# Two-group ending of each GraphSAGE layer's last half, with sums in four PSUM banks, early aggregation of the other batch-norm statistics, and some maskings moved behind the batch norm

## Chip, cores and metric

One Trainium2 chip, one core. The metric is device time in microseconds (us) of one execution; the time before is the median of 3 runs.

## What is computed

The input is x (16 graphs, 1024 nodes, 128 features), an adjacency matrix of 1024 x 1024 per graph and a node mask. Two layers, each with a residual: x = x + layer(relu(layernorm(x))). The first is masked multi-head attention. The second is a GraphSAGE stack of three layers over a thinned ("dilated") adjacency; its core in the reference is

```python
def _sage(x, adj, Wr, Wx, b, mf):
    deg = jnp.clip(jnp.sum(adj, axis=-1, keepdims=True), 1.0, None)
    agg = jnp.einsum('bij,bjd->bid', adj, x) / deg
    out = agg @ Wr + x @ Wx + b
    nrm = jnp.maximum(jnp.linalg.norm(out, axis=-1, keepdims=True), NORM_EPS)
    return out / nrm * mf[..., None]

def _bn(x, g, b):
    m = jnp.mean(x, axis=(0, 1))
    v = jnp.var(x, axis=(0, 1))
    return (x - m) * jax.lax.rsqrt(v + BN_EPS) * g + b
...
h1 = _bn(jax.nn.relu(_sage(x, adj_d, Wr1, Wx1, b1, mf)), g1, be1)
h2 = _bn(jax.nn.relu(_sage(h1, adj_d, Wr2, Wx2, b2, mf)), g2, be2)
h3 = _bn(jax.nn.relu(_sage(h2, adj_d, Wr3, Wx3, b3, mf)), g3, be3)
xc = jnp.concatenate([h1, h2, h3], axis=-1) * mf[..., None]
return (xc @ Wl + bl) * mf[..., None]
```

The batch norm takes mean and variance over all 16 graphs and 1024 nodes, so no row of a layer can enter the next one before the last row's statistics are known. That is the point in the program that the change rewrites, three times, once per layer.

## The kernel before, in words

The function `swept` does all the work here (a second function, `walked`, runs only when a flag says that the first one's way of thinning has not settled; the profile shows none of it). Up to about 2340 us it computes the attention and the thinning of the adjacency, and leaves the transposed adjacency (`aT_d`, f32) and the marks of removed edges (`mr_d`, bf16) in HBM. Then come the three GraphSAGE layers (L = 0, 1, 2, called first, second and third layer in the text), and behind them a tail that adds the third layer's part of the output.

A layer is a loop over 16 graphs (b) with two halves (c = 0, 1) of 512 nodes each; one half is a turn. In a turn i the generator `nodes` (L1107) makes, in this order:

- the half's own product h @ Wx with the bias in PSUM (`own`, L1118), copied to SBUF by ScalarE (`mine`, L1123);
- the sums over neighbours, aT.T @ y with y = h @ Wr (y is written by `given`, L1098, product `pn`, L1103): four tiles of 128 nodes, eight products each, in the PSUM tile `pg` of two banks, two tiles to a bank (L1132). In the first layer a column of ones in y gives the degree too;
- the ending: 1/degree (L1143 and L1146, first layer only), `o = pg / degree + mine` (L1150, one instruction per tile), the squares of all four tiles on ScalarE (L1155), their sums (L1158), maximum (L1160), root on ScalarE (L1161), reciprocal and node mask (L1163, L1164), relu times factor (L1165), four transposes by TensorE into the bank `pt` (L1169), statistics for the batch norm (`bn_stats`, L1176, or L1172 for the last half) and a copy to SBUF (`hT`, L1173).

The ending of one half is spread over the turn of the next one. The order on TensorE, VectorE and ScalarE is written out by hand in the loop from L1230 on (`tc.manual_schedule`): generators stop at named points, and `go(before, "norm")` runs the ending of the half before up to such a point between two blocks of sums (`go(this, "sums")`). Among them stand the four maskings of the next turn's adjacency (`pieces`, L146, VectorE: aT is set to zero where an edge was removed; each takes two of the eight blocks of rows), the next graph's batch norm (`incoming`, L1096, ScalarE) and products. In the second and third layer, turns with c = 1 also add the finished layer's part of the output (`output_part`, products L1059, additions L1064); for the last two graphs these four parts are kept back until the layer's end (`held`, `last_parts`), where TensorE has nothing else to do.

SP's queue loads each turn's adjacency (`edges`, L133, 2 MB into one of four buffers) and marks (L137, two of 512 KB into one of four buffers each) up to three turns ahead; a load waits until its buffer's last reader is done, and those behind it in the queue wait too. Its order, and that of GpSimd's queue (`sums_so_far`, the stores of partial outputs), is the scheduler's.

At a layer's end (L1318 to L1336) the last half's ending runs with nothing beside it but the held products. Then `bn_aggr` takes all 32 groups of statistics (L1325), ScalarE the root (L1328), and VectorE makes scale and shift (`affine`, L1329 to L1332). The next layer begins with the batch norm of graph 0 (`incoming`, both halves on ScalarE), `given` for both halves, and its first turn. After the third layer the tail (from L1338) loads the partial outputs, and per graph takes the batch norm (`come`), eight products (L1364), eight additions (six on VectorE, L1372, two by way of ScalarE, L1401, and VectorE, L1385) and two stores by SP (L1378).

PSUM tags in the text: `sc` is the tile of two banks (two buffers: `pg` lives there), `o`, `t`, `n` and `y` are single banks for `own`, `pt`, `pn` and the output parts.

## Time and profile before

| | |
|---|---|
| median of 3 runs | 3398.16 us (3393.99, 3398.16, 3398.21) |
| the profiled execution's own time | 3396.91 us |
| its span, first to last instruction | 3395.1 us |
| mean granted clock of TensorE | 0.995 |
| TensorE, VectorE, ScalarE busy | 98%, 89%, 68% |
| DMA, mean over the span | 227 GB/s |
| last sums to next layer's first sums, first to second layer | 2649.4 to 2665.0 us |
| the same, second to third layer | 2994.9 to 3007.8 us |
| last sums of the third layer to the tail's first addition | 3336.3 to 3349.9 us |

How to read it: a line of the timeline gives start, duration, engine, line of the kernel, operation, what is written from what, shape and count, and in brackets how long the engine had been idle before and what released it. PE is TensorE, DVE is VectorE, ACT is ScalarE, SP the queue that issues most DMAs. A line of windows gives a stretch, its length, and the busy time of each engine with the number of instructions, then the clock that TensorE was granted (1.00 is full), the share of the DMA engines that was busy, and GB/s. Matmuls in f32 count two records per product, transposes one. Shares of busy time are means over stages with different limits; what a change at a layer's end is worth is read there.

### The profile page before, as it was taken

How to read it: one execution, taken by the hardware profiler on the slowest of the kernel's cores; microseconds unless marked ns; L12 is line 12 of the kernel's file. 1: busy time of each engine (PE TensorE's matmuls, PEld its weight loads, DVE VectorE, ACT ScalarE, POOL GpSimd, SP SyncE). 2: the span in 40 equal slices, each digit the busy share in tenths (PEclk: the TensorE clock that was granted, in tenths of full speed). 3: DMA queues.
4: the chain of work that ended last, by engine and by line, in shares of the span. 5: the costliest groups of instructions: out<-in, count | busy, mean ns of one | idle time of the engine just before them, and what ended most of it. 6: DMA issues, size and time to landing. Idle time of an engine off the chain costs nothing. (4 is left out here: it accounts for less than half of the span.)

```text
span 3395.1 us, 86338 instructions
## 1 busy us (share of the span) xinstructions
PE 3310.6 (98%) x34855; PEld 1872.4 (55%) x34855; DVE 3025.5 (89%) x5399; ACT 2305.4 (68%) x3909; POOL 164.2 (5%) x253
## 2 busy tenths in 40 slices
PE   8999999999999999999999999999999899999997
PEld 3333333333333333333334334336999899999997
DVE  7898989989989998998998999897888899988887
ACT  7699689779879969968976986884232344423334
POOL 2000000000000000000000000000000000000000
PEclk9999999999999999999999999999999999999999
DMA  7357456547637736845863773677999799989996
GB/s 242 108 168 206 137 149 199 161 129 221 188 122 213 221 122 183 238 144 158 236 190 122 237 240 119 189 228 261 346 341 343 284 353 350 353 323 350 352 351 222
DMA packets 650123, 772.28 MB, mean 227 GB/s; under 512 B 173264, under 2 KB 569168, under 8 KB 637424
## 3 DMA queue, kind: packets, MB, share of 16 engines
q1 hardware_dynamic: 632672, 708.58, 64.4%
q0 software_dynamic: 15456, 57.30, 5.0%
q8 instruction: 275, 4.51, 0.6%
q14 instruction: 136, 1.11, 0.1%
q10 hardware_dynamic: 1584, 0.79, 0.1%
HBM read 508.50 MB, written 157.29 MB: 196 GB/s over the span
## 5 line engine op out<-in xcount | busy, mean ns | idle before, releaser
L603 DVE TENSOR_TENSOR w<-e,aT 128x1024 f32<-128x1024 f32 x1024 | 1205.5, 1219 | 138.4 <-ACT e L598 136.8
L598 ACT ACTIVATE e<-sc 128x1024 f32<-128x1024 f32 x1024 | 991.9, 1022 | 333.6 <-PE sc L560 332.6
L1132 PE MATMUL pg<-y,aT 128*128 128x128 f32 (+1 forms) x6144 | 729.8, 275 | 0.0
L1132 PEld LDWEIGHTS pg<-y,aT 128*128 128x128 f32 x6144 | 707.9, 192 | 0.0
L487 PE MATMUL acc<-w,both 128*32 128x512 f32 x4096 | 586.7, 605 | 3.1 <-DVE w L603 2.6
L560 PE MATMUL sc<-qT,kT 32*128 32x512 f32 x4096 | 584.4, 640 | 0.3 <-ACT qT L315 0.3
L492 PE MATMUL acc<-e,eps 128*32 128x512 f32 x4096 | 573.1, 592 | 0.0
L146 DVE SCALAR_TENSOR_TENSOR aT<-mr,aT 128x1024 f32<-128x1024 bf16 x384 | 458.8, 1217 | 0.0
L492 PEld LDWEIGHTS acc<-e,eps 128*32 128x32 f32 x4096 | 150.6, 110 | 294.6 <-issue 289.6
L1155 ACT ACTIVATE sq<-o 128x512 f32<-128x512 f32 x96 | 60.6, 631 | 328.5 <-DVE o L1150 328.5
L554 PEld LDWEIGHTS <-never 32*32 32x32 bf16 x8192 | 80.9, 88 | 347.9 <-issue 325.6
L554 PE MATMUL sc<-nomask,never 32*32 32x512 bf16 x8192 | 252.3, 385 | 16.8 <-ACT e L598 12.3
L1173 ACT COPY hT<-pt 128x512 f32<-128x512 f32 x96 | 56.3, 586 | 289.3 <-PE pt L1169 280.0
L560 PEld LDWEIGHTS sc<-qT,kT 32*128 32x128 f32 x4096 | 160.1, 183 | 116.9 <-issue 116.1
L505 PEld LDWEIGHTS pa<-ident,a 128*128 128x128 f32 x1024 | 107.7, 141 | 181.4 <-issue 129.7
L487 PEld LDWEIGHTS acc<-w,both 128*32 128x32 f32 x4096 | 92.8, 108 | 156.2 <-issue 65.4
L915 ACT ACTIVATE wr<-both,th 128x512 f16<-128x512 f16 x256 | 172.1, 730 | 7.1 <-DVE both L900 6.9
L505 PE MATMUL pa<-ident,a 128*128 128x128 f32 x1024 | 168.3, 287 | 6.4 <-DMA a<-in_adj 5.7
L512 ACT ACTIVATE nomask<-aT 128x512 bf16<-128x512 f32 x256 | 161.4, 630 | 8.1
L1150 DVE SCALAR_TENSOR_TENSOR o<-pg,rdeg,mine 128x128 f32<-128x128 f32 x384 | 108.1, 344 | 55.9 <-PE pg L1132 52.6
L508 ACT COPY aT<-pa 128x512 f32<-128x512 f32 x256 | 152.7, 597 | 5.3 <-PE pa L505 4.3
L900 DVE TENSOR_TENSOR_SCAN both<-rk 128x513 f16<-128x513 bf16 x128 | 155.9, 1218 | 0.0
(228 smaller groups left out, 3894.9 us busy)
## 6 DMA issues: line engine op xcount, KB each, us to landing
aT<-aT_d SPq DMA_DIRECT2D x94, 2048.0 KB, 9.9
mr<-mr_d SPq DMA_DIRECT2D x188, 512.0 KB, 6.0
aT_d<-aT SPq DMA_DIRECT2D x256, 256.0 KB, 4.0
a<-in_adj SPq DMA_DIRECT2D x253, 256.0 KB, 3.7
ad<-in_adj SPq DMA_DIRECT2D x112, 512.0 KB, 4.2
nomask<-nomask SPq DMA_DIRECT2D x512, 96.0 KB, 2.7
nomask<-nomask SPq DMA_DIRECT2D x512, 64.0 KB, 2.7
nomask<-nomask SPq DMA_DIRECT2D x512, 32.0 KB, 2.7
```

The costliest lines, as they stand in the source:

```text
L146: nc.vector.scalar_tensor_tensor(part, mrs[h][:, j : j + 2, :].rearrange("p j n -> p (j n)"), 0.0, part, ALU.is_equal, ALU.mult)
L487: nc.tensor.matmul(acc[g][32 * j : 32 * j + 32, :], v1[:, m, (2 * j + g) * HW : (2 * j + g) * HW + 32], ws[j // 2][:, j % 2, :], start=(m ...
L492: nc.tensor.matmul(acc[g][32 * j : 32 * j + 32, :], eps8, es[j // 2][:, j % 2, :], start=False, stop=(m == NB - 1),)
L505: nc.tensor.transpose(pa[:, k * P : (k + 1) * P], a[:, k, :], ident)
L512: nc.scalar.activation(nomask[:, 0, :], aT[:, 0, :], AF.Relu, bias=1.0, scale=-1e38, accum_out=zeros[:, i : i + 1])
L554: nc.tensor.matmul(scs[j // 2][to : to + 32, j % 2, :], never[rows, rows], nomask[rows, j, :], start=True, stop=False, tile_position=(32 * ...
L560: nc.tensor.matmul(scs[j // 2][:, j % 2, :], kT[rows, mm], qTs[c][rows, g, :], start=False, stop=True, tile_position=(32 * j, 0),)
L598: nc.scalar.activation(e, scs[q], AF.Exp, scale=1.0 / math.sqrt(HD))
L603: nc.vector.tensor_tensor(w, es[q], aT.to_broadcast([P, 2, HN]), ALU.mult)
L900: nc.vector.tensor_tensor_scan(pair_sums[b % 2], row[:, 0::2], row[:, 1::2], 0.0, ALU.add, ALU.add)
L915: nc.scalar.activation(wrs[b][:, t * HN : (t + 1) * HN], pair_sums[b % 2][:, t : t + HN], AF.Abs, bias=at[:, b : b + 1], scale=2.0,)
L1132: nc.tensor.matmul(pg[:, i // 2, at : at + width], aT[:, j, i * P : (i + 1) * P], y[:, j, :width], start=(j == 0), stop=(j == NB - 1),)
```

## The change

- The last turn of a layer (graph 15, c = 1) has its four tiles' sums in four different banks instead of two: the two of `pg`, one of the other `sc` buffer, and `y`.
- Its ending is a new generator, `ending`, in two groups of two tiles. Tiles 0 and 1 are scaled after the second block of sums, tile 2 after the third, and the first group is normed while TensorE works on the last block; tile 3 follows. Squares and their sums come from one instruction per tile with an accumulator (ScalarE for tiles 0 to 2, VectorE for tile 3). Each group has its own two transposes and its own statistics.
- The half before it (c = 0 of graph 15) is normed, transposed and counted earlier in that turn; then its and all other halves' statistics, 31 groups, are aggregated (`most`) and multiplied with their share of the rows. After the last two groups' statistics, the two results are combined by formula (share 1 - 0.5/16).
- Of the four maskings of the next layer's first turn, three (end of the first layer) or two (end of the second) are moved from the last turn behind the affine (`owed`). The third layer's end has none.
- The batch norm of the next layer's graph 0 (`arrive`) is made right there, the first half in two quarters on ScalarE, the second half on VectorE. One of the four held output parts is added before the owed maskings, three after.
- The held parts 2 and 3 of the products share one `sc` tile (`late["pair"]`) instead of taking two.
- At the end of the first layer, where there are no held parts, TensorE makes 14 and then 18 transposes of the identity into an unused bank (`running`).
- The constant `bn_eps` and its memset go: epsilon is in `most`.

On SP's queue two loads change places: at the end of the first layer the adjacency of turn 35 now stands ahead of the marks of turn 34, and at the end of the second one load of marks stands one place later. Away from the layer ends every engine has the same order as before.

The core of the diff (left out: the removal of `bn_eps`, the tile sizes of `stats` and `two`, and `come(0)`, which `arrive` replaces):

```diff
     banks = {"n": (ps_d, "d"), "o": (ps_o, "acc0"), "t": (ps_o, "acc1"), "y": (ps_m, "m")}
 
     def bank(name, tag):
+        if tag in (0, 1):
+            if tag == 0:
+                late["pair"] = ps_s.tile([P, 2, 512], F32, name=name, tag="sc")
+            return late["pair"][:, tag, :]
         if tag == "g":
             return ps_s.tile([P, 2, 512], F32, name=name, tag="sc")[:, 0, :]
         where, tag = banks[tag]
...
             cc = slice(c * HN, (c + 1) * HN)
             nc.scalar.activation(hT[:, cc], hTs[b][:, cc], AF.Identity, bias=affine[:, 1:2], scale=affine[:, 0:1])
 
+    def arrive(hT, b, affine):
+        for cc in (slice(0, HN // 2), slice(HN // 2, HN)):
+            nc.scalar.activation(hT[:, cc], hTs[b][:, cc], AF.Identity, bias=affine[:, 1:2], scale=affine[:, 0:1])
+        nc.vector.tensor_scalar(hT[:, HN:], hTs[b][:, HN:], affine[:, 0:1], affine[:, 1:2], ALU.mult, ALU.add)
+
     def given(L, b, c, hT, tag="n"):
 
         pn = bank(f"pn_{L}_{b}_{c}", tag).rearrange("p (k d) -> p k d", d=D)
...
 
         mine = evict() if late else None
         pg = ps_s.tile([P, 2, 512], F32, name=f"pg_{L}_{b}_{c}", tag="sc")
+        if last_half:
+            pgs = [pg[:, 0, :], pg[:, 1, :], bank(f"pg_{L}_2", "g"), bank(f"pg_{L}_3", "y")]
+        else:
+            pgs = [pg[:, i // 2, (i % 2) * (D + 1) :] for i in range(HB)]
         for i in range(HB):
             for j in range(NB):
-                at = (i % 2) * (D + 1)
                 nc.tensor.matmul(
-                    pg[:, i // 2, at : at + width], aT[:, j, i * P : (i + 1) * P], y[:, j, :width],
+                    pgs[i][:, :width], aT[:, j, i * P : (i + 1) * P], y[:, j, :width],
                     start=(j == 0), stop=(j == NB - 1),
                 )
             yield "sums"
+            if last_half and i == 1:
+                end = ending(L, k0, pgs, mine)
+                go(end, "first group")
+            if last_half and i == 2:
+                go(end, "third block")
+        if last_half:
+            yield from end
+            return
         if not mine:
             mine = evict()
             yield "mine"
...
         pt = bank(f"pt_{L}_{b}_{c}", "t")
         for i in range(HB):
             nc.tensor.transpose(pt[:, i * P : (i + 1) * P], o[:, i, :], ident)
-        last_half = b == B - 1 and c == 1
-        if last_half:
+        if b == B - 1:
             nc.vector.bn_stats(late["stats"][:, 2 * b + c, :], pt)
         nc.scalar.copy(hTs[b][:, c * HN : (c + 1) * HN], pt)
         yield "transposed"
-        if not last_half:
+        if b < B - 1:
             nc.vector.bn_stats(late["stats"][:, 2 * b + c, :], pt)
         yield "end"
+
+    def ending(L, k0, pgs, mine):
+
+        pool, small, rdeg = late["pool"], late["small"], late["rdeg"]
+        o = pool.tile([P, HB, D], F32, name=f"o_{L}_end", tag="o")
+        sq = pool.tile([P, HB, D], F32, name=f"sq_{L}_end", tag="sq")
+        f = small.tile([P, HB], F32, name=f"f_{L}_end", tag="f")
+
+        def scaled(i):
+            dg = rdeg[:, k0 + i : k0 + i + 1]
+            if L == 0:
+                nc.vector.tensor_scalar(dg, pgs[i][:, D : D + 1], 1.0, None, ALU.max)
+                nc.vector.reciprocal(dg, dg)
+            nc.vector.scalar_tensor_tensor(o[:, i, :], pgs[i][:, :D], dg, mine[:, i, :], ALU.mult, ALU.add)
+
+        def squared(i):
+            if i < 3:
+                nc.scalar.activation(sq[:, i, :], o[:, i, :], AF.Square, accum_out=f[:, i : i + 1])
+            else:
+                nc.vector.scalar_tensor_tensor(
+                    sq[:, i, :], o[:, i, :], 1.0, o[:, i, :], ALU.mult, ALU.mult, accum_out=f[:, i : i + 1]
+                )
+
+        def root(two):
+            nc.vector.tensor_scalar(f[:, two], f[:, two], NORM_EPS**2, None, ALU.max)
+            nc.scalar.activation(f[:, two], f[:, two], AF.Sqrt)
+
+        def normed(two):
+            nc.vector.reciprocal(f[:, two], f[:, two])
+            nc.vector.tensor_tensor(f[:, two], f[:, two], mf[:, k0 + two.start : k0 + two.stop], ALU.mult)
+            nc.vector.scalar_tensor_tensor(o[:, two, :], o[:, two, :], 0.0, last(f[:, two], D), ALU.max, ALU.mult)
+
+        def turned(two):
+            for i in range(two.start, two.stop):
+                nc.tensor.transpose(pt[:, i * P : (i + 1) * P], o[:, i, :], ident)
+
+        def counted(two):
+            nc.vector.bn_stats(late["two"][:, two.start // 2, :], pt[:, two.start * P : two.stop * P])
+
+        first, second = slice(0, 2), slice(2, 4)
+        for i in range(2):
+            scaled(i)
+            squared(i)
+        yield "first group"
+        scaled(2)
+        squared(2)
+        root(first)
+        normed(first)
+        yield "third block"
+        pt = bank(f"pt_{L}_end", "t")
+        turned(first)
+        scaled(3)
+        squared(3)
+        root(second)
+        counted(first)
+        normed(second)
+        yield "result"
+        turned(second)
+        counted(second)
+        nc.scalar.copy(hTs[B - 1][:, HN:], pt)
+        yield "end"
+
+    def running(L, n):
+
+        idle = bank(f"idle_{L}_{n}", "n")
+        for i in range(n):
+            nc.tensor.transpose(idle[:, (i % HB) * P : (i % HB + 1) * P], ident, ident)
 
     turns = [(L, b, c) for L in range(3) for b in range(B) for c in range(2)]
 
...
         hT, last_rows = attend()
         next(last_rows)
         nothing = lambda: None
+        SHARE = 1.0 - 0.5 / B
+        hs = {}
         for L in range(3):
             if L > 0:
                 new_stats(L)
-                hT = shared.tile([P, N], F32, name=f"h_{L}_0", tag="ad", bufs=2)
-                for c in range(2):
-                    incoming(L, 0, c, hT, affine)
+                hT = hs.pop(0)
                 for c in range(2):
                     whole(given(L, 0, c, hT))
             before = None
 
-            held, last_parts = ["o", "g", "g", "y"], []
+            held, last_parts = ["o", 0, 1, "y"], []
             for b in range(B):
                 more = b + 1 < B
                 if more:
...
                             next(last_rows)
                     if biased:
                         next(biased)
+                    last_half = b == B - 1 and c == 1
                     pieces[0]()
                     if before:
                         go(before, "norm")
+                    if last_half:
+                        go(before, "result")
+                        now = 1 if L == 0 else 2
+                        owed, pieces = pieces[now:], pieces[:now] + [nothing] * 4
                     pieces[1]()
-                    if before:
+                    if before and not last_half:
                         go(before, "result")
                     beside[1]()
                     go(this, "sums")
...
                             next(last_rows)
                     if biased:
                         next(biased)
-                    turn_later = before and (c == 0 or L == 0)
+                    turn_later = before and (c == 0 or L == 0) and not last_half
                     if before and not turn_later:
                         go(before, "transposed")
-                    pieces[2]()
-                    pieces[3]()
-                    if before and not turn_later:
+                    if last_half:
                         go(before, "end")
+                        most = late["small"].tile([P, 4], F32, name=f"most{L}", tag="most", bufs=2)
+                        nc.vector.bn_aggr(most[:, 0:2], late["stats"])
+                        nc.vector.tensor_scalar(most[:, 2:3], most[:, 0:1], SHARE, None, ALU.mult)
+                        nc.vector.tensor_scalar(most[:, 3:4], most[:, 1:2], SHARE, BN_EPS, ALU.mult, ALU.add)
+                    else:
+                        pieces[2]()
+                        pieces[3]()
+                        if before and not turn_later:
+                            go(before, "end")
                     go(this, "sums")
                     if turn_later:
                         go(before, "transposed", "end")
...
                     fetch_h0(b + 2)
                 if more:
                     hT = hTn
-            go(before, "scaled")
+            go(before, "result")
             for part in last_parts[:2]:
                 next(part)
-            go(before, "norm", "result", "transposed", "end")
+            if L == 0:
+                running(L, 14)
+            go(before, "end")
             for part in last_parts[2:]:
                 next(part)
-            mv = late["small"].tile([P, 3], F32, name=f"mv{L}", tag="mv", bufs=2)
-            nc.vector.bn_aggr(mv[:, 0:2], late["stats"])
+            if L == 0:
+                running(L, 18)
+            mv = late["small"].tile([P, 5], F32, name=f"mv{L}", tag="mv", bufs=2)
+            gain, shift = late["norms"][:, L, 0:1], late["norms"][:, L, 1:2]
+            nc.vector.bn_aggr(mv[:, 0:2], late["two"])
+            nc.vector.tensor_tensor(mv[:, 2:3], mv[:, 0:1], most[:, 0:1], ALU.subtract)
+            nc.vector.scalar_tensor_tensor(
+                mv[:, 2:3], mv[:, 2:3], SHARE * (1.0 - SHARE), mv[:, 2:3], ALU.mult, ALU.mult
+            )
+            nc.vector.scalar_tensor_tensor(mv[:, 1:2], mv[:, 1:2], 1.0 - SHARE, mv[:, 2:3], ALU.mult, ALU.add)
 
             affine = late["small"].tile([P, 2], F32, name=f"affine{L}", tag="affine", bufs=2)
-            nc.scalar.activation(mv[:, 1:2], mv[:, 1:2], AF.Sqrt, bias=bn_eps)
-            nc.vector.scalar_tensor_tensor(mv[:, 2:3], mv[:, 0:1], -1.0, late["norms"][:, L, 0:1], ALU.mult, ALU.mult)
-            nc.vector.reciprocal(mv[:, 1:2], mv[:, 1:2])
-            nc.vector.tensor_tensor(affine[:, 0:1], late["norms"][:, L, 0:1], mv[:, 1:2], ALU.mult)
-            nc.vector.scalar_tensor_tensor(
-                affine[:, 1:2], mv[:, 2:3], mv[:, 1:2], late["norms"][:, L, 1:2], ALU.mult, ALU.add
-            )
-            for part in last_parts:
+            nc.scalar.activation(mv[:, 3:4], mv[:, 1:2], AF.Sqrt, bias=most[:, 3:4])
+            nc.vector.scalar_tensor_tensor(mv[:, 4:5], mv[:, 0:1], 1.0 - SHARE, most[:, 2:3], ALU.mult, ALU.add)
+            nc.vector.scalar_tensor_tensor(mv[:, 4:5], mv[:, 4:5], -1.0, gain, ALU.mult, ALU.mult)
+            nc.vector.reciprocal(mv[:, 3:4], mv[:, 3:4])
+            nc.vector.tensor_tensor(affine[:, 0:1], gain, mv[:, 3:4], ALU.mult)
+            nc.vector.scalar_tensor_tensor(affine[:, 1:2], mv[:, 4:5], mv[:, 3:4], shift, ALU.mult, ALU.add)
+            hs[0] = shared.tile([P, N], F32, name=f"h_{L + 1}_0", tag="ad", bufs=2)
+            arrive(hs[0], 0, affine)
+            whole(last_parts[0] if last_parts else ())
+            for piece in owed:
+                piece()
+            for part in last_parts[1:]:
                 whole(part)
 
         outs = []
```

More of the change, by code (lines that the diff above doesn't have):

```diff
@@ L153, in swept @@
     mf2 = const.tile([P, B * NB], F32, name="mf2")
-    bn_eps = const.tile([P, 1], F32, name="bn_eps")
-    nc.vector.memset(bn_eps, BN_EPS)
     minus_half = const.tile([P, NB], F32, name="minus_half")
@@ L1207, in new_stats @@
     def new_stats(L):
-        late["stats"] = late["small"].tile([P, 2 * B, 6], F32, name=f"stats{L}", tag="stats", bufs=2)
+        late["stats"] = late["small"].tile([P, 2 * B - 1, 6], F32, name=f"stats{L}", tag="stats", bufs=2)
+        late["two"] = late["small"].tile([P, 2, 6], F32, name=f"two{L}", tag="two", bufs=2)
     p1 = ctx.enter_context(ExitStack())
@@ L1273, in swept @@
                         next(biased)
+                    last_half = b == B - 1 and c == 1
                     pieces[0]()
@@ L1343, in swept @@
             outs.append(tile_)
-        hs = {}
         def come(b):
@@ L1386, in finish @@
             leave(b, 1)
-        come(0)
         come(1)
```

## The prediction

> **What bounds the kernel now.** I read the page, then who waited for whom inside the three layers, then the timeline at each layer's end, then the granted clock by windows.
>
> ```profile
> PE 3310.6 (98%) x34855; PEld 1872.4 (55%) x34855; DVE 3025.5 (89%) x5399; ACT 2305.4 (68%) x3909; POOL 164.2 (5%) x253
> ```
>
> TensorE (PE) is busy 98% of 3395.1 us. The layers run from about 2340 to 3345 us; there TensorE's whole list of waits (in total, times, longest) is:
>
> ```profile
> PE pt L1169 <- DVE o L1165: 11.1, 4, 4.7
> PE pn L1103 <- ACT h L1096: 4.3, 2, 3.5
> PE pn L1103 <- ACT y L1105: 1.4, 2, 0.7
> PE ht L1086 <- ACT h L1088: 0.5, 1, 0.5
> ```
>
> No DMA and no masking is among them: inside a layer only fewer matmuls would help, and the change leaves those alone. Nearly all of these 17 us falls at the layer ends, where the batch norm needs the last half. The second layer's end shows the chain:
>
> ```profile
> 2990.72 0.63 PE L1169 MATMUL pt<-ident,o 128*128 128x128 f32 x4 [1.26 <-DVE o L1165]
> ...
> 2994.96 1.12 DVE L1150 SCALAR_TENSOR_TENSOR o<-pg,rdeg,mine 128x128 f32<-128x128 f32 x4 [1.51 <-PE pg L1132]
> 2996.18 0.63 ACT L1155 ACTIVATE sq<-o 128x512 f32<-128x512 f32 x1 [4.21 <-DVE o L1150]
> 2996.84 0.69 DVE L1158 TENSOR_REDUCE f<-sq 128x4 f32<-128x512 f32 x1 [0.76 <-ACT sq L1155]
> ...
> 2999.25 1.08 PE L1169 MATMUL pt<-ident,o 128*128 128x128 f32 x4 [2.54 <-DVE o L1165]
> ...
> 3001.11 1.02 DVE L1325 BATCH_NORM_AGGREGATE mv<-stats 128x2 f32<-128x192 f32 x1
> ...
> 3002.77 0.21 DVE L1332 SCALAR_TENSOR_TENSOR affine<-mv,norms 128x1 f32<-128x1 f32 x1
> ...
> 3003.88 1.16 PE L1103 MATMUL pn<-weights,h 128*128 128x128 f32 x8 [0.72 <-ACT h L1096]
> ```
>
> Sums end at 2994.93; the affine is written at 3002.98, and the next layer's first product starts 8.95 us after the sums. At the first layer's end it is 9.27 us (2649.37 to 2658.64), and there the clock is half:
>
> ```profile
> 2654.27:2657.68 3.41, 0.83 (x4) 0.42 (x3) 2.28 (x7) 0.88 (x2) 0.00 (x0) 0.50 0.73 308
> 2657.68:2661.10 3.42, 2.08 (x8) 1.78 (x8) 3.42 (x5) 1.87 (x3) 0.00 (x0) 0.50 0.01 2
> 2661.10:2664.51 3.41, 3.12 (x13) 2.97 (x14) 1.18 (x2) 1.24 (x3) 0.00 (x0) 0.51 0.74 214
> 3002.43:3005.84 3.41, 2.01 (x16) 1.63 (x15) 3.31 (x15) 2.14 (x4) 0.50 (x1) 1.00 0.01 5
> ```
>
> After the times, their length and a comma stands TensorE's busy time; the third number from the right is the clock. The clock changes only on a grid of 3.41 us. It fell after stretches with 0.16, 1.11, 1.18, 1.35 and 1.62 us of TensorE work, held after 1.93 and 2.01, and rose after 3.10 to 3.18 but not after 2.08. The first layer's eight products (pn) cost 2.08 us there, 1.16 at the second's end.
>
> **The change, part by part.** Rows used: a narrow VectorE (DVE) step that needs the one before takes 0.16 to 0.18 us and starts every 0.20 (L1163, L1164, L1165 at 2998.01, 2998.22, 2998.41); L1150's tiles start every 0.27 and last 0.34.
>
> *Earlier end of the first half (c = 0).* In the last turn the norm of the half before goes ahead of the second masking, and its transposes stand after two blocks of sums in every layer. Second layer: TensorE idles 1.26 us at 2990.72, since L1165 waited behind a masking of 1.22 us. Without that, the reciprocal starts as ACT's root is there (2988.71), L1165 ends 2989.81 and the transposes start 2989.95: the sums end 0.77 earlier, at 2994.16. Third layer: no maskings, nothing changes. First layer: the transposes come eight products earlier than before, TensorE is ready at 2645.30, the result at 2645.56: 0.4 to 0.5 us lost, sums end 2649.85.
>
> *The chain, second layer.* VectorE behind the first half's result: one masking to 2990.95; statistics 0.70 to 2991.65; the 31 groups aggregated ahead, 1.0 (L1325's 1.02 for 32); two narrow steps, 2993.0. Then three tiles' sums at 0.28 each (2993.85); they have been ready in their own banks since 2992.3, so VectorE, not TensorE, is late. ACT squares a tile with its sum in 0.41 (L699: 0.31, its accumulator read of 0.19 starting 0.22 in), so the first root comes at 2994.6; reciprocal, mask and result over 256 columns end 2995.45. Only then the last tile: scaled 2995.73 (1.6 behind the sums), squared 2996.1, maximum 2996.3, root on ACT 2996.55 with the first group's statistics beside it to 2996.67; normed 2997.5. TensorE does the 16 held products (1.95) after the first two transposes, to 2997.64, then the other two, to 2998.0. Statistics over 256 columns 2998.45; aggregation of two groups 0.18 (L276: 0.173); three narrow steps, 2999.26; ACT root 0.30; three steps: affine 3000.13. ACT's first quarter of h takes 0.6, so the product starts at about 3000.88 against 3003.88: **3.0 us less**.
>
> *First layer.* The same list with two more steps per tile (degree, reciprocal, 0.4) and only one masking ahead: VectorE is at the last tile 2.1 us after the sums; affine at 2657.1 against 2657.74, product at 2657.8 against 2658.64: 0.8 less. The rest is the clock. Before, the products at half clock make 6.32 us from the first product to the next layer's sums (2658.64 to 2664.96); at full clock it is 3.94 (3003.88 to 3007.82): 2.4 less if the clock holds. 14 and 18 transposes of the identity (L1169 at 0.115 each, 1.6 and 2.1 us) fill the two waits. TensorE is idle from 2649.85 to 2652.15; a grid stretch that covers this has some 1.1 us of work, so the clock falls in half or more of the positions, and 11 or so of the 14 then run at 0.25 and delay the second transposes by about 1.0; that full stretch brings the clock back. So 3.2 less without the fall, 2.2 with it; I take **2.5**.
>
> *Third layer and tail.* VectorE begins the three tiles at 3334.85, reaches the last tile 0.9 after the sums (3336.33), affine 3341.97 against 3344.39. Then 16 additions of the held products (4.22 us) and the tail's first addition. Before, it waited for TensorE until 3349.90, because those products needed a bank that the additions free; now the bank is free already (held products share one tile), TensorE has 4 us, and the first addition starts 3346.75: **3.1 less**. The tail's 36.2 us is VectorE's and moves along whole.
>
> *Maskings behind the norm.* Three (first layer) and two (second), one every 1.17 us, end at 2661.3 and 3004.2, ahead of the next sums at 2661.75 (2.5 taken: 2662.4) and 3004.8. Their cover is the products; without it each masking would cost 1.17. In SP's queue the mask loads (mr) for two turns on wait for them, with later adjacency loads behind: issued 12 us later than now, landing 6.0 us later (median), 2667.5, used by the turn's maskings from about 2673.5. Nothing is late.
>
> *Not seen before, with both ends.* Statistics over 256: 0.28 (L274, 128 columns) to 0.70 (L1172), taken 0.42, on the path twice; result over 256: 0.34 to 0.69, taken 0.42 near L407's 0.425, twice; VectorE's square with sum: 0.26 (L716, bf16) to 0.43 (L1150 plus a read of 0.08), taken 0.33; a quarter of h: 0.39 (L1049) to 0.81 (L1096), taken 0.6; VectorE's half of h, 0.57 (L924) to 0.69, hidden behind the first y copy. Together 0.7 less to 1.4 more per layer; over three layers the sum lies 2.2 lower to 4.1 higher. The memset removed lies at the start, beside loads: nothing.
>
> **Sum.** 2.5 + 3.0 + 3.1 = 8.6 off the profiled execution's own 3396.91 (span 3395.1): 3388.3. That execution lies 1.25 below the median of the runs shown; I keep 3388.3.
>
> [...] The stretch 2999.01 to 3002.43 raised the clock with 3.18 us of work, 0.9 of it transposes; at the kernel's start a stretch with 2.73 us (12.38 to 15.79) did not, for two products (pq) behind it took 1.91, later 1.12. So transposes count here: without them 2.3 would have raised what 2.73 did not. [...]
>
> **Rivals.**
> *A: the idle transposes don't hold the clock.* Then 14 and 18 of them at 0.25 (3.5 and 4.5 us) stand ahead of the real work in TensorE's order, the first layer's next sums come 1.0 to 2.3 late, say 1.6, instead of 2.5 early: 3388.3 + 4.1 = 3392.4. The mixed windows above speak against it; no window of transposes alone speaks for. 0.12.
> *B: VectorE becomes the bound.* It is late at every layer's last tile already. On the path from the first half's statistics to the affine stand 14 narrow steps, 22 in the first layer, 50 in all. If each cost the 0.44 of a step that another engine releases (L1163: 0.27 idle and 0.17) instead of 0.20, 12.0 goes: 3.4 slower, 3400.3. It decides from 0.17 more per step on. The starts of L1163 to L1165 speak against it. 0.05.
> *C: the tail's output DMA, not VectorE, sets the end.* The DMA share there is 0.7 to 1.03; if the stores end no earlier, 3.1 goes: 3391.4. Against: SP's stores waited 22.1 us for VectorE. 0.08.
> *D: slower, by the loads held in SP's queue.* If the two mask loads land one behind the other behind an adjacency load (9.9 + 6.0 + 6.0 = 21.9 us after their issue) instead of within 6.0, they miss their turn, 12 us after the issue, by 9.9 in each of two layers: 19.8 - 8.6 = 11.2 slower, 3408.1. It decides from 16.3 us of landing on. Against: the adjacency load ahead is issued as the sums end and has landed by then (at most 11.2 us there), and TensorE never waited for a load. 0.05.
>
> Forecast 0.70. Range 3384.0 to 3394.5: the terms' ends (3386.1 and 3392.4, A and C inside), widened on each side by half the runs' spread of 4.2; B and D are left out. A difference under 0.2% (6.8 us) can't be told from none here. Faster 0.67 (the forecast, less 0.03 for its slow end); same 0.27 (that, A, C, B, less 0.01); slower 0.06 (D, and that 0.01).
>
> **What would show it.** Right: first product of the next layer 8 to 9 us (first layer) and 6.7 (second) after the sums, its eight products in 1.1 us, no TensorE wait for DVE aT, first addition of the tail about 10.4 us after the sums. Wrong: a wait of pg for aT, windows of 0.50 from the idle transposes on, or narrow steps over 0.3 apart.

## The result, and the profile after

| | before | after |
|---|---|---|
| median | 3396.59 us (6 runs, 3393.99 to 3402.16) | 3384.65 us (6 runs, 3381.13 to 3386.87) |
| profiled execution: own time, span, clock | 3396.91, 3395.1, 0.995 | 3385.60, 3383.8, 0.998 |

The ratio of the times is 0.9962 (95% interval 0.9949 to 0.9975). The forecast was 3388.3, so the time is 3.7 us below it; by the medians the gain is 11.9 us, where 8.6 was forecast.

The page's line of busy time:

```profile
PE 3305.9 (98%) x34887; PEld 1869.4 (55%) x34887; DVE 3030.7 (90%) x5446; ACT 2305.5 (68%) x3927; POOL 163.9 (5%) x253
```

TensorE has 32 instructions more (the idle transposes) and is busy 4.7 us less: at the layer ends it no longer runs at half clock (granted on average 1.00 in 2640 to 2665, 2987 to 3010 and 3334 to 3350 us; before 0.79, 0.92 and 0.80 in 2640.5 to 2665, 2986.5 to 3008 and 3334 to 3351). Its waits in the layers (in total, times, longest):

```profile
PE pt_end L1230 <- DVE o_end L1226: 2.4, 3, 1.2
PE pt_end L1230 <- DVE rdeg L1207: 1.9, 1, 1.9
PE pn L1110 <- ACT h L1102: 1.9, 2, 1.0
PE pn L1110 <- ACT y L1112: 1.4, 2, 0.7
PE pt L1188 <- DVE o L1184: 0.8, 2, 0.5
PE ht L1088 <- ACT h L1090: 0.5, 1, 0.5
```

11.1 us of waits for the normed result (`o`) became 5.1 (first, second and fifth line), and no line has `aT`: the owed maskings hold nothing up. The second layer's end, from the timeline:

```profile
2987.91 0.86 DVE L1209 SCALAR_TENSOR_TENSOR o_end<-pg,rdeg,mine 128x128 f32<-128x128 f32 x3
2988.35 0.31 ACT L1213 ACTIVATE sq_end<-o_end 128x128 f32<-128x128 f32 x1 [1.01 <-DVE o_end L1209]
...
2988.66 0.29 ACT L1213 ACTIVATE sq_end<-o_end 128x128 f32<-128x128 f32 x1
...
2990.25 0.34 DVE L1209 SCALAR_TENSOR_TENSOR o_end<-pg,rdeg,mine 128x128 f32<-128x128 f32 x1
...
2992.51 0.38 PE L1230 MATMUL pt_end<-ident,o_end 128*128 128x128 f32 x2
...
2993.39 0.21 DVE L1428 BATCH_NORM_AGGREGATE mv<-two 128x2 f32<-128x12 f32 x1
...
2994.82 0.21 DVE L1441 SCALAR_TENSOR_TENSOR affine<-mv,norms 128x1 f32<-128x1 f32 x1
...
2995.72 1.20 PE L1110 MATMUL pn<-weights,h 128*128 128x128 f32 x8 [1.04 <-ACT h L1102]
```

The sums end at 2989.33. Three tiles are scaled before that; the affine is written 5.70 us after it (8.05 before), the next layer's product starts 6.4 after it (8.95 before). The last tile is scaled 0.92 late, as VectorE is still at the first group. ACT squares a tile every 0.31 us (starts at 2988.35 and 2988.66): the read of the accumulator, 2988.56 to 2988.75, overlaps the next square. The first layer's end, by windows:

```profile
2651.30:2654.71 3.41, 3.10 (x29) 2.87 (x28) 2.60 (x14) 0.86 (x3) 0.00 (x0) 1.00 0.99 423
2654.71:2658.13 3.42, 1.88 (x15) 1.45 (x13) 3.25 (x7) 1.90 (x4) 0.00 (x0) 1.00 0.19 77
```

The clock is 1.00 in both where it was 0.50 before. At the third layer's end the first addition of the tail comes 10.1 us after the sums (13.6 before).

**One measure for all runs.** In the rest, an *end* is the time from the start of the last half's own product (the bias product ahead of L1118, here L1126) to the next layer's first sums, or to the tail's first addition. *Start* is when the first layer's end begins: what lies ahead of it. From an end to the next the layers take 319.66 us in both kernels, and the tail 36.1 to 36.2.

| profile | start | first | second | third |
|---|---|---|---|---|
| before | 2640.52 | 24.44 | 23.20 | 22.43 |
| after | 2639.33 | 20.79 | 19.92 | 18.97 |
| again (after's kernel) | 2638.29 | 21.53 | 19.94 | 18.98 |
| no_idle | 2638.15 | 23.59 | 19.94 | 18.98 |
| only_idle | 2640.74 | 21.70 | 25.57 | 22.31 |
| masks_ahead | 2637.04 | 24.55 | 23.69 | 18.97 |
| late_most | 2637.96 | 23.02 | 19.94 | 19.22 |
| two_banks | 2635.80 | 25.50 | 25.94 | 23.38 |
| one_group | 2633.86 | 20.24 | 19.75 | 19.02 |
| one_group_late_most | 2636.03 | 23.48 | 22.37 | 20.04 |
| one_group_timed | 2640.19 | 20.23 | 19.75 | 19.02 |
| after_timed, after_timed_2 | 2635.95, 2635.43 | 21.94, 21.96 | 21.57, 21.58 | 18.98, 18.97 |
| before_again, _third, _fourth | 2641.93, 2640.03, 2638.42 | 24.78, 24.81, 24.98 | 23.22, 23.19, 22.76 | 22.22, 22.17, 20.73 |
| eps_back, eps_back_2 | 2640.70, 2640.49 | 20.79, 20.80 | 19.92, 19.93 | 18.97, 18.97 |
| eps_back_timed, place_kept | 2644.03, 2642.61 | 20.82, 20.81 | 21.33, 21.57 | 18.97, 18.98 |

Between the two profiled executions 11.3 us went: 3.65, 3.28 and 3.46 at the ends and 1.2 ahead of them, less 0.3 after the tail. The theory for the ends is that of the prediction; the open question was what lies ahead of them.

### The profile page after: what moved, and what is told of

The parts are those of the page before. It is cut to its first block, busy times and chain, and to the rows that moved or that the text cites. A ratio compares the mean times of both kernels' runs of the same rounds, so it can differ in the third digit from the quotient of the medians.

```text
span 3383.8 us, 86469 instructions
## 1 busy us (share of the span) xinstructions
PE 3305.9 (98%) x34887; PEld 1869.4 (55%) x34887; DVE 3030.7 (90%) x5446; ACT 2305.5 (68%) x3927; POOL 163.9 (5%) x253
## 4 chain that ended last, share of the span: by engine, by line
PE 65%; DVE 18%; ACT 9%; DMA 5%; issue 2%; SPq 1%; ACTq 0%; POOL 0%; DVEq 0%
PE pg L1143 19%; PE sc L558 9%; PE acc L485 8%; DVE w L601 8%; PE acc L490 7%; ACT e L596 4%; PE sc L552 3%; PE pn L1110 2%; PE own L1126 2%; PE pa L503 2%; DMA nomask<-nomask 2%; PE py L1061 2%; PE pt L1188 1%; DVE both L898 1%; DVE er L922 1%
```

## The experiments

**again**: after's kernel, unchanged.

> The changed kernel itself once more. The measure in this and the other runs is the stretch from the last turn's own product (L1126, first record of its bias product) to the next layer's first sums, or to the tail's first addition: 24.44, 23.20 and 22.43 us before, 20.79, 19.92 and 18.97 in the changed kernel's profile. My theory (the gain sits in these three stretches, and the clock's grid lies differently in each execution): second and third stretch the same within 0.1; the first 20.8 if the clock holds again, up to 1.0 more if it falls in TensorE's wait. Rival (the clock can't fall with the idle transposes there): all three within 0.1. The rest, up to the first layer's end, may differ by a few us either way by the theory that it is chance from run to run.

3384.73 us. The second and third ends repeat within 0.02. In the first, 14 idle transposes took 2.73 us instead of 1.69: by that length the clock fell, and the end is 0.74 longer. So one and the same end takes different times (20.79 and 21.53 us). In before's profile the granted clock changes eleven times, always a whole multiple of 3.41 us apart; that this grid lies elsewhere in each execution is an estimate from such lengths.

**no_idle**: the idle transposes taken out.

```diff
-            if L == 0:
-                running(L, 14)
             go(before, "end")
...
-            if L == 0:
-                running(L, 18)
```

> The changed kernel without the 14 and 18 idle transposes at the first layer's end. Theory (they hold the clock, and that is 2.4 us of the first stretch): a clock of 0.50 from about 2656, eight products in about 2.1 us instead of 1.2, first stretch 22.8 to 23.2 instead of 20.79; the other two unchanged. Rival (transposes don't count for the clock, or the clock doesn't matter): first stretch 20.8, clock as with them.

The first end takes 23.59, 2.8 more and above the 23.2 expected, all of it behind the affine (7.45 instead of 4.67 to the next sums; the chain takes 6.75 either way), and 0.48 more goes in the turn behind it. Its products run at half clock, by their length:

```profile
2651.71 0.44 PE L1230 MATMUL pt_end<-ident,o_end 128*128 128x128 f32 x2 [1.84 <-DVE o_end L1226]
2654.98 2.08 PE L1110 MATMUL pn<-weights,h 128*128 128x128 f32 x8 [2.83 <-ACT h L1102]
2657.74 2.08 PE L1110 MATMUL pn<-weights,h 128*128 128x128 f32 x8 [0.68 <-ACT y L1112]
```

The same product is 1.20 long in the kernel after. The idle transposes are worth about 3 us.

**only_idle**: the kernel before with 40 and 29 idle transposes, and nothing else of the change.

```diff
-            go(before, "norm", "result", "transposed", "end")
+            go(before, "norm", "result")
+            if L == 0:
+                running(L, 40)
+            go(before, "transposed", "end")
+            if L == 0:
+                running(L, 29)
```

> The kernel before, with idle transposes alone added at the first layer's end (40 behind the last sums, 29 behind the real transposes, enough to fill the two waits of 4.7 and 3.5 us). Theory: the clock holds at 1.00, the eight products take 1.1 to 1.2 us instead of 2.08, first stretch 22.0 to 22.2 instead of 24.44; others 23.2 and 22.4 as before. Rival (transposes don't count): clock falls all the same, the idle transposes run at 0.25 each and the first stretch is 24.4 or longer, up to 32.

The first end takes 21.70, 2.74 less than before (a little better than expected): most of what the whole change brings there.

```profile
2649.43 4.53 PE L1183 MATMUL idle<-ident 128*128 128x128 f32 x40
2654.34 0.63 PE L1169 MATMUL pt<-ident,o 128*128 128x128 f32 x4 [0.37 <-DVE o L1165]
2654.80 3.33 PE L1183 MATMUL idle<-ident 128*128 128x128 f32 x29
2658.51 1.16 PE L1103 MATMUL pn<-weights,h 128*128 128x128 f32 x8 [0.38 <-ACT h L1096]
```

For 4.53 us TensorE does nothing but transposes of the identity, longer than one stretch of the grid (3.41), and each of the 40 takes 0.113 us, where in the kernel after, at a granted clock of 1.00, 14 took 1.69 (0.12 each). The real products behind the other 29 take 1.16 us instead of 2.08. So at this end transposes alone held the clock. That refutes rival A. The time was still 3397.39 us: in this execution the clock fell at the second layer's end, whose code is before's, and that end took 25.57 (its first products 2.08 us instead of 1.16).

**masks_ahead**: all four maskings ahead of the norm again.

```diff
-                        now = 1 if L == 0 else 2
+                        now = 4
...
                         go(before, "end")
+                        pieces[2]()
+                        pieces[3]()
```

> The changed kernel with all four maskings of the next layer's first turn ahead of the norm again, in the last turn. Theory (VectorE is late at the last tile, so whatever stands ahead of it there delays the affine one for one): first stretch longer by 3 x 1.17 = 3.5 (24.3), second by 2 x 1.17 = 2.3 (22.3), third the same 18.97. Rival (VectorE had room there): 20.8 and 19.9, within 0.3.

3390.58 us. First end 24.55, near the 24.3 expected; third 18.97 as it was. The second is 1.4 longer than expected (23.69). TensorE there:

```profile
2987.05 3.74 PE L1143 MATMUL pg<-y,aT 128*128 128x128 f32 x32
2994.09 0.61 PE L1230 MATMUL pt_end<-ident,o_end 128*128 128x128 f32 x2 [3.29 <-DVE o_end L1226]
2994.49 3.42 PE L1061 MATMUL py<-weights,h 128*128 128x128 f32 x16
2997.75 0.38 PE L1230 MATMUL pt_end<-ident,o_end 128*128 128x128 f32 x2
```

The maskings hold VectorE by their 2.34 us; TensorE idles 3.29 (1.16 in the kernel after), and the 16 held products take 3.42 instead of 1.95, by which the clock fell, with the second transposes queued behind them. Here the longer wait cost twice: itself, 2.13 us, and 1.47 in the products behind it.

**late_most**: the 31 groups aggregated behind the last transposes, as the kernel before does it.

```diff
 # these three lines moved from the last turn to just ahead of the aggregation of the last two groups
 nc.vector.bn_aggr(most[:, 0:2], late["stats"])
 nc.vector.tensor_scalar(most[:, 2:3], most[:, 0:1], SHARE, None, ALU.mult)
 nc.vector.tensor_scalar(most[:, 3:4], most[:, 1:2], SHARE, BN_EPS, ALU.mult, ALU.add)
```

> The changed kernel with the aggregation of the 31 groups and its two narrow steps put back behind the last statistics (1.16 us of VectorE from 2645.91 to 2647.07 in the first layer). Theory (VectorE comes 1.7, 0.9 and 0.7 us late to the last tile because of what stands ahead of it, this aggregation among it): it gains ahead what it loses behind, so the three stretches grow by only 0 to 0.2, 0.2 to 0.4 and 0.4 to 0.6. Rival (aggregating ahead is worth its whole length): 1.16 more in each.

From the sums to the affine it is 0.25 shorter (first layer), the same (0.02) and 0.24 longer. At the first end it took 7.15 from the affine to the next sums (4.67 in the kernel after), which makes the 23.02; that the clock fell there is an estimate from no_idle, where that stretch took 7.45 with products at half clock. So neither the theory's growth (0 to 0.6) nor the rival's 1.16: beside two groups, aggregating ahead gains next to nothing, as its 1.0 us stands in VectorE's way before the last group as much as behind it.

**two_banks**: all four tiles' sums in `pg`, two to a bank, the rest as it is.

```diff
-        if last_half:
-            pgs = [pg[:, 0, :], pg[:, 1, :], bank(f"pg_{L}_2", "g"), bank(f"pg_{L}_3", "y")]
-        else:
-            pgs = [pg[:, i // 2, (i % 2) * (D + 1) :] for i in range(HB)]
+        pgs = [pg[:, i // 2, (i % 2) * (D + 1) :] for i in range(HB)]
```

> The changed kernel with the last turn's sums in two banks of two tiles each, as in all other turns. Theory (VectorE reaches tile 2 only as the last sums end, so a bank of its own gives it little): stretches longer by 0 to 0.4, the most in the second and third layer, where tile 2 is scaled 0.8 to 1.2 us ahead of the sums' end. Rival (separate banks are what lets the ending begin ahead): nothing can be scaled before all sums end, 1.7 to 2.5 longer in each.

3396.87 us; both theories were wrong about where. The sums themselves end 6.3, 5.4 and 5.2 us later, and what follows is shorter. In the first layer:

```profile
2644.98 3.66 PE L1140 MATMUL pg<-y,aT 128*128 128x129 f32 x16 [3.37 <-DVE o_end L1206]
...
2648.68 0.16 DVE L1204 TENSOR_SCALAR rdeg<-pg 128x1 f32<-128x1 f32 x1 [3.75 <-PE pg L1140]
...
2649.47 2.05 PE L1140 MATMUL pg<-y,aT 128*128 128x129 f32 x16 [0.83 <-DVE o_end L1206]
```

The third and fourth blocks now wait for VectorE's reads of tiles 0 to 2, and VectorE for the blocks, and the first block back, behind 3.37 us of waiting, takes 3.66 for its 16 records, where the next takes 2.05: by its length it runs at half clock. The built program holds these waits as semaphores: users of one PSUM tile are put in order. It goes by the tile and not by the bank: the third block writes the second bank of `pg`, and waits for VectorE's reads of tiles 0 and 1, which lie in the first. So tiles of their own are what lets this ending begin beside sums. Without them an end is 4.4 to 4.7 us longer (6.0 at the second, 1.6 of it put down to the clock, an estimate from the 1.65 of after_timed below), and longer than before's. Whether the chip would need those waits wasn't tried.

**one_group**: one ending of four tiles instead of two of two, with all else kept.

```diff
+        group = slice(0, 4)
         for i in range(2):
             scaled(i)
             squared(i)
         yield "first group"
         scaled(2)
         squared(2)
-        root(first)
-        normed(first)
         yield "third block"
         pt = bank(f"pt_{L}_end", "t")
-        turned(first)
         scaled(3)
         squared(3)
-        root(second)
-        counted(first)
-        normed(second)
+        root(group)
+        normed(group)
         yield "result"
-        turned(second)
-        counted(second)
+        turned(group)
+        nc.vector.bn_stats(late["two"][:, 0, :], pt)
...
-            nc.vector.bn_aggr(mv[:, 0:2], late["two"])
+            nc.vector.bn_aggr(mv[:, 0:2], late["two"][:, 0:1, :])
```

> The changed kernel with one group of four tiles instead of two of two: tiles 0 to 2 are still scaled and squared as their sums come, but maximum, root, reciprocal, mask, relu, transposes and statistics are made once for all four after the last tile. Theory (the first group's own steps are what makes VectorE late to the last tile): stretches shorter, by 0.7, 0.3 and 0.1: 20.1, 19.6, 18.9. Rival (two groups shorten the chain, since half of the norm is done ahead): 0.4 to 1.0 longer in each.

From the sums to the affine 0.56 and 0.17 less, and 0.04 more. Beside the early aggregation two groups don't pay: norming the first is four steps of VectorE and a wait for ACT's root, and the last tile waits behind them.

**one_group_late_most**: both edits.

> One group, and the aggregation of the 31 groups behind the last statistics. Theory: with one group VectorE waits for the last sums, so the early aggregation is free there and its delay costs its whole length: 1.1 to 1.2 more than with one group alone in the second and third stretch, and 0.7 to 1.2 in the first. Rival (aggregation costs the same with one or two groups): whatever late_most cost against the changed kernel.

Against one_group the same stretch is 0.77, 1.01 and 1.02 longer. With one group VectorE is free when the last tile comes, and aggregating ahead is worth its 1.0 us. The four runs together give the stretch from the sums to the affine, summed over the three ends, with each idea and without:

| | one group | two groups |
|---|---|---|
| aggregation behind | 20.02 (one_group_late_most) | 17.92 (late_most) |
| aggregation ahead | 17.22 (one_group) | 17.91 (after) |

Each idea alone gains (2.1 and 2.8 us), but both together gain no more than two groups alone, and less than the aggregation alone. (The rest of 23.48 and 22.37, 2.5 and 1.6 us more than in one_group, is put down to the clock, an estimate: its mean is 0.997 here and 0.998 in one_group.)

**one_group_timed** and **after_timed**, on one chip:

> The one-group ending with everything else of the change kept, timed in five rounds against the kernel before. From the three ends of its first profile (20.24, 19.75, 19.02 us from the last half's own product to the next layer's first sums, or the tail's first addition; 24.44, 23.20, 22.43 before) 11.1 us less than before: a ratio of 0.9967. If the 9 us between its one time so far and before's profile are more than chance ahead of the layers, up to 0.995. Rival, that two groups pay after all: a ratio above the changed kernel's.

> The changed kernel, unchanged, timed beside the one-group version on one chip. Theory: the ends differ by 0.7 us at most, which five rounds cannot tell from none (both 0.9955 to 0.9975). Ends in the profile again 20.8 to 21.6, 19.9, 19.0.

3386.10 us (0.9958, 0.9944 to 0.9973) and 3386.68 us (0.9960, 0.9946 to 0.9974): not told apart. In after_timed the clock fell at the first and second ends, by the lengths (14 idle transposes 3.19 us instead of 1.69, the second products behind the affine 1.87 instead of 1.16): +1.15 and +1.65.

**before_again, before_third, before_fourth, eps_back, eps_back_2**: the timed gain of 12 to 13 us is more than the ends hold. Three profiles of the kernel before against two of the changed one with the removed constant put back (nothing reads it):

```diff
     mf2 = const.tile([P, B * NB], F32, name="mf2")
+    bn_eps = const.tile([P, 1], F32, name="bn_eps")
+    nc.vector.memset(bn_eps, BN_EPS)
     minus_half = const.tile([P, NB], F32, name="minus_half")
```

> The kernel before, unchanged, a second profile. If the 1.2 us that the changed kernel's first profile was ahead before the first layer's last turn are chance, the own product of that turn starts anywhere from 2634 to 2641 (2640.5 in the first profile); if something at the start of the program is cheaper in the changed kernel, it starts at 2640 or later again. The three ends: 22.0 to 24.5, 23.2 to 25.6, 22.4, as the clock falls at the first and second or not.

> The kernel before, a third profile. Theory (chance ahead of the layers): the first layer's last turn starts its own product anywhere from 2634 to 2642 us. Rival (something at the start costs the kernel before more): 2640 or later again.

> As the third: chance says 2634 to 2642 for the start of the first layer's last turn, the rival 2640 or later again.

> The changed kernel with the constant bn_eps and its memset put back (nothing reads it; the result is the same). Theory: the own product of the first layer's last turn starts at 2634 to 2641 us, as in the changed kernel, and the three ends take 20.8 to 21.9, 19.9 to 21.6 and 19.0. Rival (the constant, its memset or the places that it moves the other tiles to cost time ahead of the layers): it starts at 2640 or later.

> As eps_back, a second profile: theory 2634 to 2641, rival 2640 or later.

Before's start came at 2641.93, 2640.03 and 2638.42, the changed kernel's with the constant at 2640.70 and 2640.49. All but the 2638.42 fit the rival, but all lie within what chance allowed too (2634 to 2642), so they settle nothing by themselves.

**eps_back_timed** and **after_timed_2**, on one chip:

> The changed kernel with the constant bn_eps and its memset put back, timed in five rounds beside the changed kernel on one chip. Theory (chance): its mean span is within 1.5 us of the changed kernel's. Rival (the constant costs time ahead of the layers): 2.5 to 3.5 us longer, and the start of the first layer's last turn again at 2640 us or later.

> The changed kernel beside eps_back_timed: theory the same mean span within 1.5 us; rival 2.5 to 3.5 us shorter, with the start of the first layer's last turn at 2634 to 2640 us.

Mean 3387.87 us (9 executions, 3385.14 to 3392.19) with the constant, 3382.83 (5, 3380.74 to 3384.44) without: no overlap, 5.0 us, more than the rival's 2.5 to 3.5. Against before 0.9970 (0.9960 to 0.9980) and 0.9958 (0.9945 to 0.9972). The rival is right: the constant costs time.

**place_kept**: its place kept in SBUF, its memset dropped.

```diff
+    bn_eps = const.tile([P, 1], F32, name="bn_eps")
     minus_half = const.tile([P, NB], F32, name="minus_half")
```

> The changed kernel with the place of bn_eps kept in SBUF and no memset. If the places of the tiles cost the 5 us: a mean of 3386.5 to 3389 us, packets of 256 bytes at 16.5 to 16.6 ns, and the first layer's last turn at 2638.4 or later. If the memset does: 3381.5 to 3384, and the last turn at 2634 to 2640; the packets at 16.5 would then show that their time does not matter.

Mean 3388.48 us (6 executions, 3385.45 to 3392.22), packets of 256 bytes at 16.5 ns, start 2642.61. All three signs named ahead speak for the place and against the memset, though on another chip than the two runs before. In the built program thousands of tiles lie 32 bytes lower per partition without the constant. Part of the time is seen in VectorE's waits of 16 to 2320 us (in total, times, longest), here in place_kept:

```profile
DVE rk L715 <- DMA gl<-mr_d: 5.3, 4, 1.9
```

and in after_timed_2:

```profile
DVE rk L714 <- DMA gl<-mr_d: 0.8, 1, 0.8
```

`gl` are marks that the thinning loads. This wait takes 1.9 to 5.3 us (mean 3.7) in the nine profiles with the place and 0 to 2.6 (mean 1.2) in the eleven without, a difference of 2.5 us where the starts differ by 4.0 (means 2641.1 and 2637.1). It holds for the means only: the starts overlap (2638.42 to 2644.03 with the place, 2633.86 to 2640.19 without, both of these from one_group's kernel), and the latest start, in eps_back_timed, goes with the shortest of the nine waits.

## Why the prediction was right, and where it was wrong

**The ends: right, and nearly in size.** Over four profiles of the kernel before the three ends take 24.75, 23.09 and 21.89 us on average, over the eight with the changed ends (after, again, after_timed, after_timed_2, the three of eps_back and place_kept) 21.18, 20.72 and 18.97. That is 3.6, 2.4 and 2.9, together 8.9, where 2.5 + 3.0 + 3.1 = 8.6 was forecast. (With the second and third end of only_idle, whose code there is before's, it is 3.6, 2.9 and 3.0, together 9.4.) That the sum is so near is in part luck: 1.1 too little in the first layer against 0.6 and 0.2 too much in the others. In the two profiled executions alone it was 10.4, as the clock fell at all three ends in before's (0.50 from 2654.27, 2999.01, 3340.35 and 3347.17 on) and at none in after's (1.00).

- *First layer, 2.5 (3.2 without a fall of the clock, 2.2 with it).* 3.65 without; 2.9 and 2.5 with it (again, after_timed). The mis-sized term is the chain: from the sums to the affine 6.73 instead of 7.25. VectorE begins the last tile 1.68 behind the sums (2650.40) and not 2.1; what follows took 5.05, as reckoned (5.15). The prediction carried the second layer's list over, in which ACT's squares lag behind; here a tile with its degree takes VectorE 0.65, and ACT waits for it at each. Ending the first half earlier cost 0.54 (0.4 to 0.5 forecast), and from the affine to the next sums it was 4.67 (4.65).
- *Second layer, 3.0.* 3.28: the sums end 0.76 earlier (0.77 forecast), the chain takes 5.70 instead of 5.97, since ACT squares every 0.31 and not 0.41, and the product 0.69 instead of 0.75 behind the affine. Not foreseen: in four of the eight profiles this end takes 21.33 to 21.58 instead of 19.92 to 19.94, so 1.4 to 1.65 comes back; the second products behind the affine took 1.87 (after_timed, after_timed_2) and 1.95 us (place_kept) there instead of 1.16, by which the clock fell.
- *Third layer, 3.1.* 3.46: affine 5.48 behind the sums (5.64), first addition 10.1 (10.4). The tail moved along whole, so rival C is refuted.
- *The parts*, each taken out of the whole by itself, so that they don't add up: without tiles of their own nothing is left of the gain (4.4 to 4.7 us an end); the idle transposes are worth 3 at the first end; the maskings 3.8 at the first two ends each, 2.34 of the second's itself and the rest the clock's; two groups or the early aggregation, each beside the other, nothing, and both together 2.1 over the three ends, where the aggregation alone brings 2.8.
- *Rival B.* Narrow steps that follow one another start every 0.20 (L1224, L1225, L1226 at 2989.51, 2989.71, 2989.91), as the prediction took it.
- *Rival D.* The two mask loads were issued 2657.20 and landed within 7.0 us; no turn waited for one.

**The failed step: "The memset removed lies at the start, beside loads: nothing."** It priced the instruction and not the place. The constant's 32 bytes a partition, in a pool under thousands of tiles, moved those tiles, and with them the places that loads up to 2340 us write to: 5.0 us in the one comparison on the same chip; over all 17 executions of after's kernel in the timed comparisons (mean 3384.63) and the 17 with the place kept (3387.98), on several chips, it is 3.3. The two findings close the sum: 8.9 to 9.4 at the ends and 3.3 to 5.0 by the place make 12.2 to 14.4; the three timed ratios of after's kernel, 0.9962, 0.9960 and 0.9958, are 12.9 to 14.3 of some 3398. With the constant left in place the change brings 0.9970 or 0.9969, 10 us, near the 8.6 forecast.

**What stays open** is how 32 bytes do it. The tiles `a`, `gl`, `gm`, `et` and most of `nomask` begin at an address of 32 modulo 256 with the constant and of 0 without; `mr` lies the other way, at 0 with it and 224 without. The waits for `gl` are longer with the constant (mean 3.7 against 1.2 us), and in these loads it is the side written to that moved; no run here shows how its place sets their time. The mean times of packets in the records don't agree throughout: in all profiles, without overlap, packets of 1,024 bytes take 52.2 to 52.3 ns with the place and 51.5 to 51.7 without, but those of 256 bytes 16.5 to 16.6 and 17.9 to 18.0. Another place (64 or 224 bytes off) wasn't tried.

## What to carry to other kernels

Here an ending that began beside the matmuls that feed it needed its inputs in PSUM tiles of their own; without that, starting early made both sides wait (TensorE 3.37 and VectorE 3.75 us at two_banks' first end). Of two measures that shorten one chain, test each alone, the two together and neither: where both lean on the same engine, the second may be worth nothing or less (17.91 us with both against 17.22 with the aggregation alone here). A removed constant was two edits: an instruction, and a shift of thousands of tiles by 32 bytes, worth 3.3 to 5.0 us, so an experiment that is to be about something else should keep the places.

## What the runs showed of the hardware

- In before's profile the granted clock changed eleven times between 1.00 and 0.50, every time a whole multiple of 3.41 us from the others (2340.24, 2343.65, 2654.27, 2664.51 and on). What an end cost differed from one execution to the next: the same end took 20.79 to 21.96 us (first) or 19.92 to 21.58 (second) in eight profiles of the same code there, and before's second end 22.76 to 25.57.
- Idle f32 transposes held the clock at one end: 40 in a row took 4.53 us in only_idle (0.113 each, where 14 took 1.69 at a granted clock of 1.00 in the kernel after), and the end 21.70 against 24.44 us.
- ACT's square with a sum was followed by the next 0.29 to 0.31 us later (2988.35, 2988.66, 2988.95 in the kernel after), though square and read of the accumulator last 0.29 to 0.31 and 0.19.
- A shift of thousands of tiles by 32 bytes in SBUF changed this kernel's time by 3 to 5 us of 3385, as much as a planned edit.
